# Splitting an image's projected rows during its own turned write pass

## The chip, the cores and the metric

The kernel runs on one core of a Trainium2 chip. The metric is the device time of one execution in microseconds (us); the three timed runs before the change give a median of 9846.35 us. One more execution was profiled: every start and duration quoted here comes from that one.

## What is computed

The input `x` is a batch of 8 images of 128x128 pixels with 128 channels. Layer 0 is a linear attention with a norm and a residual. Layer 1 is a block with a selective scan in four directions, cut here to what the change touches:

```python
xz = x @ Win                       # per pixel: 128 -> 512
xb, z = jnp.split(xz, 2, axis=-1)  # 256 channels each
xb = silu(conv3x3_depthwise(xb) + conv_b)
xf = xb.reshape(Bb, Cd, L)                               # natural order of pixels
xt = jnp.transpose(xb, (0, 1, 3, 2)).reshape(Bb, Cd, L)  # turned order
xs = jnp.stack([xf, xf[..., ::-1], xt, xt[..., ::-1]], axis=1)
x_dbl = jnp.einsum('bcl,cd->bdl', xs_flat, Wxproj)       # 256 channels -> 10 rows
dt, Bs, Cs = x_dbl[:, :8], x_dbl[:, 8:9], x_dbl[:, 9:]   # then the scan over L
```

L is 128*128 = 16384, Cd is 256. The scan needs, for each image, the silu output times B (in natural and in turned order), and the ten rows of `x_dbl` (in both orders).

## The kernel before, in words

The program has three stages on the same core, one after the other: `layer0`, `layer1_front` and `layer1_scan`. An all-engine barrier (line 713) stands between the second and the third. In the front and the scan stage `in_order` writes the order of every engine by hand: what the source calls first is first in that engine's queue, and nothing overtakes it. Nearly all DMAs are issued from SP (SyncE), in one queue.

`layer1_front` is the stage of the change. It goes over the 8 images in the order `SEQ` = 4, 6, 5, 7, 0, 1, 2, 3, and cuts each into 16 chunks of 8x128 = 1024 pixels, numbered g = 0 to 15 within the image (n over all images). `step(n)` interleaves neighbouring chunks: TensorE projects (`project`) and does two taps of the convolution (`taps_pe`), ScalarE does three taps (`taps_act`), GpSimd adds them (line 504), VectorE does the other taps (`taps_dve`, lines 510 and 512), and ScalarE applies silu into the resident tile `ures` (128 KB per partition: the whole image, both halves of the 256 channels). `rows` and `keep_rows` make the ten rows of a chunk and store them to `xds` in DRAM. `by_b` (line 549) multiplies `ures` by B and writes it in natural order. `load_sum`, `sum_d` and `store_sum` carry a sum over directions through DRAM (tile `gl`, tag `d`).

Between two images, at g = 0 of the next one, stands the turned write pass, `turn`: 32 pieces (2 channel halves of 16), each copied from `ures` with rows and columns exchanged into a tile `turned` of 128x1024 (line 622; 19 copies on VectorE, 13 on ScalarE), then written to DRAM by a DMA of 512 KB (line 623). The tiles come from two rings of buffers shared with other tiles of the stage: tag `tb` with four buffers and tag `tc` with two (every third piece). A ring hands out its buffers in the order of the calls: a new tile waits until everything that used the tile four (or two) places earlier is done, a DMA out of it included. The next image's silu overwrites `ures`, so the pass stands in every engine's path.

`split` handles half of an image's ten rows (five rows) at a time, from `load_rows`, which reads them back from `xds` as `xw`, 128x5x128, in runs of 512 B (640 of them). Five TensorE transposes (line 605, PSUM tag `pj`, one buffer, shared with `project`) and a ScalarE copy (line 607) make the turned version `xh`. `split3` (lines 43 and 45) then cuts each version into three bfloat16 parts on VectorE: cast, subtract, cast, subtract, cast. So one split has ten VectorE instructions of 128x640, and six DMAs of 160 KB to `xps` (line 613) in runs of 256 B. Before the change the two splits of an image are called at the end of the steps g = 1 and g = 2 of the next image, and the last image's two after the loop, ahead of the barrier.

Of the kernel before, what the change touches and what calls it, by code (L numbers as in the profile page):

```python
# [8 lines left out]
F32 = mybir.dt.float32  # L9
# [7 lines left out]
P = 128  # L17
B = 8
H = W = 128
L = H * W  # L20
NH, HD = 4, 32
NC2 = 2
# [7 lines left out]
CH = 1024  # L30
CW = CH // H
NCH = L // CH
# [4 lines left out]
NAT, TURN = 0, 1  # L37


def split3(nc, parts, x):  # L40

    for j in range(3):
        nc.vector.tensor_copy(parts[j], x)
        if j < 2:
            nc.vector.tensor_tensor(x, x, parts[j], ALU.subtract)
# [327 lines left out]
def layer1_front(ctx: ExitStack, tc, x1, win, conv_w, conv_b, wxp, d_par, ubs, xds, xps, gts, gs):  # L373
# [11 lines left out]
    nc = tc.nc  # L385
    const = ctx.enter_context(tc.tile_pool(name="l1c", bufs=1))
    big = ctx.enter_context(tc.tile_pool(name="l1b", bufs=1))
    wp = ctx.enter_context(tc.tile_pool(name="l1w", bufs=3))
# [34 lines left out]
    for j, d in enumerate(ON_PE):  # L423
        for c in range(NC2):
            dg = wp.tile([P, P], F32, name="dg1", tag="tb", bufs=4)
            nc.vector.tensor_scalar(dg, ident, cw[:, c, tap(*d) : tap(*d) + 1], None, ALU.mult)
            p = pm.tile([P, P], F32, name="pw", tag="m")
# [16 lines left out]
    uturn = ures.rearrange("p c (w h) -> p c h w", h=H)  # L444
# [3 lines left out]
    SEQ = (4, 6, 5, 7, 0, 1, 2, 3)  # L448

    def place_of(n):  # L450
        return SEQ[n // NCH % B], n % NCH
# [3 lines left out]
    def load(n):  # L455
        b, g = place_of(n)
        x = xins[n % 2]
        cols = CW + 1 if g < NCH - 1 else CW
        src = x1[b].rearrange("c (w h) -> c w h", h=H)[:, g * CW : g * CW + cols, :]
        nc.sync.dma_start(x[:, 0:cols, inner], src)  # L460
        if g == NCH - 1:
            nc.gpsimd.memset(x[:, CW, :], 0.0)

    def project(n, c):
        pxs[n, c] = px = pj.tile([P, CW, H], F32, name="pxb", tag="pj")
        for hf in range(2):
            nc.tensor.matmul(  # L467
                px[:, hf * 4 : hf * 4 + 4, :], wi[:, c, :], xins[n % 2][:, hf * 4 : hf * 4 + 4, inner],
                start=True, stop=True,
            )  # L470

    def place(n, c):

        g = n % NCH
        xb, old = xbs[n % 2], xbs[(n - 1) % 2]
        nc.scalar.copy(xb[:, c, 1 : CW + 1, inner], pxs.pop((n, c)))
        if g == 0:
            nc.gpsimd.memset(xb[:, c, 0, :], 0.0)
        else:
            nc.scalar.copy(old[:, c, CW + 1, inner], xb[:, c, 1, inner])  # L480
            nc.scalar.copy(xb[:, c, 0, inner], old[:, c, CW, inner])
        if g == NCH - 1:
            nc.gpsimd.memset(xb[:, c, CW + 1, :], 0.0)
# [4 lines left out]
    def taps_pe(n, c):  # L488
        accs[n, c] = acc = pa.tile([P, CW, H], F32, name="acc", tag="acc")
        for hf in range(2):  # L490
            s = slice(hf * 4, hf * 4 + 4)
            for j, (dw, dh) in enumerate(ON_PE):
                x = xins[n % 2][:, hf * 4 + dw : hf * 4 + dw + 4, 1 + dh : 1 + dh + H]
                nc.tensor.matmul(acc[:, s, :], wt[:, j, c, :], x, start=(j == 0), stop=(j == len(ON_PE) - 1))  # L494
# [13 lines left out]
    def taps_dve(n, c):  # L508
        acc = accs[n, c]
        nc.vector.tensor_tensor(acc, sums.pop((n, c)), acc, ALU.add)  # L510
        for d in ON_DVE:
            nc.vector.scalar_tensor_tensor(  # L512
                acc, at(n, c, *d), cw[:, c, tap(*d) : tap(*d) + 1], acc, ALU.mult, ALU.add
            )
# [15 lines left out]
    def keep_rows(n):  # L530
        b, g = place_of(n)
        t = xdt[n % 2]
        nc.scalar.copy(t[0:64, :], prs.pop(n))
        for hf in range(2):
            s = slice(g * CH + hf * 512, g * CH + hf * 512 + 512)
            nc.sync.dma_start(xds[b][:, s], t[32 * hf : 32 * hf + R + 2, :])

    def spread(n, hf):
        pbs[n, hf] = p = pm.tile([P, 1, 512], F32, name="pb", tag="m")
        nc.tensor.matmul(p[:, 0, :], bsel[:, hf, :], xdt[n % 2], start=True, stop=True)  # L540

    def by_b(n):

        b, g = place_of(n)
        dst = ubs[b, NAT].rearrange("c p l -> p c l")
        for hf in range(2):
            s = slice(g * CH + hf * 512, g * CH + hf * 512 + 512)
            u = ures[:, :, s]
            nc.vector.tensor_tensor(u, u, pbs.pop((n, hf)).to_broadcast([P, NC2, 512]), ALU.mult)
            nc.sync.dma_start(dst[:, :, s], u)  # L550

    def sums_at(n, c):
        b, g = place_of(n)
        i = NCH - 1 - g if b // 2 % 2 == 1 else g
        if b >= 4:
            return gts[b % 2, c, :, i].rearrange("p e q -> p (e q)")
        return gs[b % 2, c][:, i * CH : i * CH + CH]

    def load_sum(n, c):
        b, g = place_of(n)  # L560
        if b // 2 != 2:
            gls[n, c] = gl = wp.tile([P, CH], F32, name="gl", tag="d", bufs=2)
            if b // 2 == 0:
                nc.sync.dma_start(gl.rearrange("p (e q) -> p e q", e=NCH), gts[b % 2, c, :, :, g])
            else:
                nc.sync.dma_start(gl, sums_at(n, c))
# [21 lines left out]
    def store_sum(n, c):  # L588
        nc.sync.dma_start(sums_at(n, c), dus.pop((n, c)))

    half = (R + 2) // 2
    xws = {}

    def load_rows(b, i):
        r = slice(i * half, i * half + half)
        xws[b, i] = x = wp.tile([P, half, H], F32, name="xw", tag="tc", bufs=2)
        nc.sync.dma_start(x, xds[b].rearrange("r (w h) -> w r h", h=H)[:, r, :])

    def split(b, i):

        r = slice(i * half, i * half + half)
        x = xws.pop((b, i))
        pt = pj.tile([P, half, P], F32, name="ptx", tag="pj")
        for j in range(half):
            nc.tensor.transpose(pt[:, j, :], x[:, j, :], ident)
        y = wp.tile([P, half, W], F32, name="xh", tag="tc", bufs=2)
        nc.scalar.copy(y, pt)  # L607
        for order, v in ((TURN, y), (NAT, x)):
            q = wp.tile([P, 3, half, P], BF16, name="parts", tag="tb", bufs=4)
            split3(nc, [q[:, j] for j in range(3)], v)  # L610
            dst = xps[b, order].rearrange("j r (a e) -> a j r e", e=P)
            for j in range(3):
                nc.sync.dma_start(dst[:, j, r, :], q[:, j])

    def turn(dst):

        for c in range(NC2):
            for i in range(NCH):
                k = NCH * c + i
                t = wp.tile([P, CW, W], F32, name="turned", tag="tc" if k % 3 == 2 else "tb", bufs=2 if k % 3 == 2 else 4)  # L620
                copy = nc.scalar.copy if k % 5 in (1, 3) else nc.vector.tensor_copy
                copy(t, uturn[:, c, i * CW : i * CW + CW, :])
                nc.sync.dma_start(dst[c][:, i * CH : i * CH + CH], t.rearrange("p h w -> p (h w)"))

    def step(n):

        live, then, later, before = 0 <= n < N, 0 <= n + 1 < N, 0 <= n + 2 < N, 1 <= n <= N
        b, g = place_of(n)
        if live:
            taps_dve(n, 0)  # L630
        if before:
            keep_rows(n - 1)
        if then:
            project(n + 1, 1)
            place(n + 1, 1)
        if live:
            taps_pe(n, 1)
        if later:
            load(n + 2)
        if before:  # L640
            for c in range(NC2):
                store_sum(n - 1, c)
        if live:
            for c in range(NC2):
                load_sum(n, c)
        if before:
            for hf in range(2):
                spread(n - 1, hf)
        if before and g == 0:
            by_b(n - 1)  # L650
            turn(ubs[place_of(n - 1)[0], TURN])
        if then:
            taps_act(n + 1, 0)
        if live:
            silu(n, 0)
        if then:
            taps_pe(n + 1, 0)
        if later:
            project(n + 2, 0)
        if live:  # L660
            taps_dve(n, 1)
        if then:
            taps_act(n + 1, 1)
        if before and g != 0:
            by_b(n - 1)
        if live:
            silu(n, 1)
        if later:
            place(n + 2, 0)
        if live:  # L670
            rows(n)
            sum_d(n)
        if n >= NCH and g in (1, 2):
            split(place_of(n - NCH)[0], g - 1)
        if n >= NCH and g in (0, 1):
            load_rows(place_of(n - NCH)[0], g)

    with in_order(tc):
        for n in range(-2, N + 1):
            step(n)  # L680
        for i in range(2):
            if i == 1:
                load_rows(SEQ[-1], 1)
            split(SEQ[-1], i)


@with_exitstack
# [497 lines left out]
```

## Time and profile before

| what | us |
|---|---|
| three timed runs: lowest, median, highest | 9833.42, 9846.35, 9846.51 |
| the profiled execution, its own time | 9824.87 |
| its span (first to last instruction on the core) | 9823.0 |
| VectorE busy in the span | 8276.1 |
| ScalarE busy, GpSimd busy, TensorE busy | 7129.7, 7184.2, 6386.5 |
| front stage, first convolution step to the end of the last turned copy | 2391 to 4946 |
| first VectorE instruction behind the barrier | 4976.70 |

A row of the timeline reads: start, duration, engine, line, operation, output<-input, shapes, count, and in brackets how long the engine had been idle and what it waited for. Rows that follow one another on one line of code are merged. A row of the table by windows reads: the window, its length, busy time and number of instructions of each engine, the TensorE clock granted, the mean busy share of the 16 DMA engines (1.0 is full) and the bytes per second.

### The profile page before, as it was taken

How to read it: one execution, taken by the hardware profiler on the slowest of the kernel's cores; microseconds unless marked ns; L12 is line 12 of the kernel's file. 1: busy time of each engine (PE TensorE's matmuls, PEld its weight loads, DVE VectorE, ACT ScalarE, POOL GpSimd, SP SyncE). 2: the span in 40 equal slices, each digit the busy share in tenths (PEclk: the TensorE clock that was granted, in tenths of full speed). 3: DMA queues.
4: the chain of work that ended last, by engine and by line, in shares of the span. 5: the costliest groups of instructions: out<-in, count | busy, mean ns of one | idle time of the engine just before them, and what ended most of it. 6: DMA issues, size and time to landing. Idle time of an engine off the chain costs nothing. (4 is left out here: it accounts for less than half of the span.)

```text
span 9823.0 us, 89967 instructions
## 1 busy us (share of the span) xinstructions
PE 6386.5 (65%) x24352; PEld 3135.3 (32%) x24352; DVE 8276.1 (84%) x8676; ACT 7129.7 (73%) x8226; POOL 7184.2 (73%) x4352
## 2 busy tenths in 40 slices
PE   8999999988787678667823544636345363553636
PEld 5555555553232223222300311404123040220403
DVE  6557775566898889888979999999999999999996
ACT  5556565556887788777778788887877878787784
POOL 3444554455484578667759899898998989889897
PEclk9999999999898889888955765757557585665857
DMA  2332233323666678877664957759587684866858
GB/s 91 129 131 97 86 118 131 129 101 132 219 221 214 219 265 228 243 248 263 232 197 152 253 177 202 234 164 263 154 223 207 176 257 152 246 185 191 239 153 215
DMA packets 1034807, 1851.21 MB, mean 188 GB/s; under 512 B 274852, under 2 KB 500772, under 8 KB 1026112
## 3 DMA queue, kind: packets, MB, share of 16 engines
q1 hardware_dynamic: 999488, 1711.23, 53.4%
q0 software_dynamic: 34816, 134.23, 7.1%
q8 instruction: 199, 3.26, 0.1%
q14 instruction: 304, 2.49, 0.1%
HBM read 1153.03 MB, written 692.12 MB: 188 GB/s over the span
## 5 line engine op out<-in xcount | busy, mean ns | idle before, releaser
L882 POOL TENSOR_TENSOR ubt<-ubt,sp 128x1024 f32<-128x1024 f32 x1024 | 2451.4, 2441 | 186.3 <-ACT sp L875 159.5
L871 PE MATMUL px<-rows,dtw 128*128 128x512 bf16 x2048 | 948.3, 564 | 2251.9 <-DVE y L941 1011.9
L504 POOL TENSOR_TENSOR tap<-tap 128x1024 f32<-128x1024 f32 x512 | 1206.2, 2366 | 720.7 <-ACT tap L502 614.7
L512 DVE SCALAR_TENSOR_TENSOR acc<-xb,cw,acc 128x1024 f32<-128x1024 f32 x1024 | 1320.7, 1290 | 51.1
L494 PE MATMUL acc<-xi,wt 128*128 128x512 f32 x2048 | 984.3, 625 | 570.8 <-ACT ures L519 570.5
L875 ACT ACTIVATE sp<-px 128x1024 f32<-128x1024 f32 x1024 | 1035.0, 1023 | 405.8 <-PE px L871 263.8
L948 POOL TENSOR_TENSOR y<-y,ubt 128x512 f32<-128x512 f32 x768 | 1160.6, 1548 | 146.4 <-DVE ubt L922 142.8
L871 PEld LDWEIGHTS <-dtw 128*128 128x128 bf16 x2048 | 167.5, 110 | 3071.4 <-issue 963.9
L889 DVE TENSOR_TENSOR_SCAN ubt<-px,state,ubt 128x1024 f32<-128x1024 f32 x480 | 1106.0, 2335 | 4.9 <-issue 3.6
L891 DVE TENSOR_TENSOR_SCAN ubt<-px,state,ubt 128x1024 f32<-128x1024 f32 x480 | 1104.6, 2335 | 6.0 <-issue 3.6
L879 ACT ACTIVATE px<-sp,sa 128x1024 f32<-128x1024 f32 x1024 | 1103.3, 1109 | 6.1
L502 ACT ACTIVATE tap<-xb,cw 128x1024 f32<-128x1024 f32 x768 | 833.2, 1139 | 155.4 <-DVE acc L510 92.4
L875 ACT ACT_TABLE_LOAD x512 | 656.9, 1283 | 223.7 <-PE px L871 205.8
L274 POOL TENSOR_TENSOR q<-q,qs 128x512 f32<-128x512 f32 x256 | 270.9, 1058 | 674.0 <-DVE qs L273 672.8
L494 PEld LDWEIGHTS acc<-xi,wt 128*128 128x128 f32 x2048 | 395.8, 199 | 1139.0 <-ACT ures L519 676.0
L879 ACT ACT_TABLE_LOAD x512 | 656.9, 1283 | 9.0
L1013 PEld LDWEIGHTS px<-wg,z 128*128 128x128 f32 x4096 | 586.3, 228 | 163.9 <-issue 157.9
L905 PE MATMUL pc<-rows,csel 128*128 128x512 bf16 x1024 | 515.9, 584 | 128.0 <-DVE rstd L1001 125.2
L1013 PE MATMUL px<-wg,z 128*128 128x128 f32 x4096 | 585.3, 312 | 0.0
L467 PE MATMUL pxb<-xi,wi 128*128 128x512 f32 x1024 | 497.4, 608 | 29.1 <-ACT xh L607 24.7
L941 DVE TENSOR_TENSOR y<-y,px 128x1024 f32<-128x1024 f32 x384 | 468.6, 1220 | 14.2
L922 DVE TENSOR_TENSOR ubt<-ubt,pc 128x1024 f32<-128x1024 f32 x384 | 466.2, 1214 | 0.0
(158 smaller groups left out, 15026.4 us busy)
## 6 DMA issues: line engine op xcount, KB each, us to landing
ubt<-ubs SPq DMA_DIRECT2D x512, 1024.0 KB
zs<-z SPq DMA_DIRECT2D x512, 256.0 KB
ubs<-ures SPq DMA_DIRECT2D x256, 512.0 KB
ubs<-turned SPq DMA_DIRECT2D x256, 512.0 KB
y<-gs POOLq DMA_DIRECT2D x128, 1024.0 KB, 11.9
z<-zs SPq DMA_DIRECT2D x256, 512.0 KB
rows<-xps SPq DMA_DIRECT2D x1536, 60.0 KB
xi<-x SPq DMA_DIRECT2D x120, 576.0 KB
```

What stands on the lines that cost most here:

```text
L494: nc.tensor.matmul(acc[:, s, :], wt[:, j, c, :], x, start=(j == 0), stop=(j == len(ON_PE) - 1))
L502: nc.scalar.activation(t, at(n, c, *d), AF.Copy, scale=cw[:, c, tap(*d) : tap(*d) + 1])
L504: nc.gpsimd.tensor_tensor(sums[n, c], sums[n, c], t, ALU.add)
L512: nc.vector.scalar_tensor_tensor(acc, at(n, c, *d), cw[:, c, tap(*d) : tap(*d) + 1], acc, ALU.mult, ALU.add)
L871: nc.tensor.matmul(p[:, hf * 512 : hf * 512 + 512], sl.dw[:, c * P : c * P + P], src, start=True, stop=True)
L875: nc.scalar.activation(t, da[n, c], AF.Softplus)
L879: nc.scalar.activation(da[n, c], sp[n, c], AF.Exp, scale=sa[:, sl.s, c : c + 1])
L882: nc.gpsimd.tensor_tensor(ubt[n][:, c, :], ubt[n][:, c, :], sp.pop((n, c)), ALU.mult)
L889: nc.vector.tensor_tensor_scan(e[:, ::-1], x[:, ::-1], e[:, ::-1], start, ALU.mult, ALU.add)
L891: nc.vector.tensor_tensor_scan(e, x, e, start, ALU.mult, ALU.add)
L948: nc.gpsimd.tensor_tensor(v[:, c], v[:, c], h[:, c], ALU.add)
L1013: nc.tensor.matmul(po[:, w, :], z[:, c, w * H : w * H + H], wg[:, c, :], start=(c == 0), stop=(c == NC2 - 1))
```

## The change

`turn` becomes `leave(b)`. It first calls `load_rows` for both halves of the image that it is about to write, then makes the same 32 pieces, and calls `split(b, 0)` behind piece 9 and `split(b, 1)` behind piece 19. The calls of `load_rows` and `split` at the end of the steps, and the code behind the loop, go. Two buffers move with it: `xw` uses the ring `d` (two buffers, that of `gl`) and `xh` the ring `tb`; `parts` stays in `tb`. Because `xw` now holds the ring `d` during the pass, `load_sum` of the step g = 0 is called after the pass and no longer ahead of it. The number of instructions, their shapes and the bytes moved are the same.

```diff
     def load_rows(b, i):
         r = slice(i * half, i * half + half)
-        xws[b, i] = x = wp.tile([P, half, H], F32, name="xw", tag="tc", bufs=2)
+        xws[b, i] = x = wp.tile([P, half, H], F32, name="xw", tag="d", bufs=2)
         nc.sync.dma_start(x, xds[b].rearrange("r (w h) -> w r h", h=H)[:, r, :])
...
-        y = wp.tile([P, half, W], F32, name="xh", tag="tc", bufs=2)
+        y = wp.tile([P, half, W], F32, name="xh", tag="tb", bufs=4)
...
-    def turn(dst):
-
-        for c in range(NC2):
-            for i in range(NCH):
-                k = NCH * c + i
-                t = wp.tile([P, CW, W], F32, name="turned", tag="tc" if k % 3 == 2 else "tb", bufs=2 if k % 3 == 2 else 4)
-                copy = nc.scalar.copy if k % 5 in (1, 3) else nc.vector.tensor_copy
-                copy(t, uturn[:, c, i * CW : i * CW + CW, :])
-                nc.sync.dma_start(dst[c][:, i * CH : i * CH + CH], t.rearrange("p h w -> p (h w)"))
+    def leave(b):
+
+        for i in range(2):
+            load_rows(b, i)
+        for k in range(NC2 * NCH):
+            c, i = divmod(k, NCH)
+            t = wp.tile([P, CW, W], F32, name="turned", tag="tc" if k % 3 == 2 else "tb", bufs=2 if k % 3 == 2 else 4)
+            copy = nc.scalar.copy if k % 5 in (1, 3) else nc.vector.tensor_copy
+            copy(t, uturn[:, c, i * CW : i * CW + CW, :])
+            nc.sync.dma_start(ubs[b, TURN][c][:, i * CH : i * CH + CH], t.rearrange("p h w -> p (h w)"))
+            if k % 10 == 9 and k < 20:
+                split(b, k // 10)
...
-        if live:
+        if live and g != 0:
             for c in range(NC2):
                 load_sum(n, c)
...
         if before and g == 0:
             by_b(n - 1)
-            turn(ubs[place_of(n - 1)[0], TURN])
+            leave(place_of(n - 1)[0])
+        if live and g == 0:
+            for c in range(NC2):
+                load_sum(n, c)
...
-        if n >= NCH and g in (1, 2):
-            split(place_of(n - NCH)[0], g - 1)
-        if n >= NCH and g in (0, 1):
-            load_rows(place_of(n - NCH)[0], g)
 
     with in_order(tc):
         for n in range(-2, N + 1):
             step(n)
-        for i in range(2):
-            if i == 1:
-                load_rows(SEQ[-1], 1)
-            split(SEQ[-1], i)
```

## The prediction, made before the changed kernel was seen

> **What bounds the kernel now.** I read the page first, then the timeline of VectorE around the end of an image, then the table by windows, then the tail of the stage.
>
> ```profile
> span 9823.0 us, 89967 instructions
> ...
> PE 6386.5 (65%) x24352; PEld 3135.3 (32%) x24352; DVE 8276.1 (84%) x8676; ACT 7129.7 (73%) x8226; POOL 7184.2 (73%) x4352
> ```
>
> VectorE (DVE) has most work, but a share over the span says nothing of one stage, so I look at the front alone. First VectorE in the first image, where no split is called, then at the same place of the second image, where one is:
>
> ```profile
> 2404.57 1.23 DVE L510 TENSOR_TENSOR acc<-tap,acc 128x1024 f32<-128x1024 f32 x1 [0.33 <-PE acc L494]
> ...
> 2413.44 1.23 DVE L510 TENSOR_TENSOR acc<-tap,acc 128x1024 f32<-128x1024 f32 x1 [2.28 <-PE acc L494]
> ...
> 2419.95 2.35 DVE L549 TENSOR_TENSOR ures<-ures,pb 128x1024 f32<-128x1024 f32 x2
> 2422.21 1.22 DVE L510 TENSOR_TENSOR acc<-tap,acc 128x1024 f32<-128x1024 f32 x1
> ```
> ```profile
> 2717.53 2.35 DVE L549 TENSOR_TENSOR ures<-ures,pb 128x1024 f32<-128x1024 f32 x2
> 2723.24 1.08 DVE L43 CAST parts<-xh 128x640 bf16<-128x640 f32 x1 [3.37 <-issue]
> 2724.35 2.86 DVE L45 TENSOR_TENSOR xh<-xh,parts 128x640 f32<-128x640 f32 x1
> 2727.24 0.49 DVE L43 CAST parts<-xh 128x640 bf16<-128x640 f32 x1
> 2727.77 0.82 DVE L45 TENSOR_TENSOR xh<-xh,parts 128x640 f32<-128x640 f32 x1
> ...
> 2732.27 1.22 DVE L510 TENSOR_TENSOR acc<-tap,acc 128x1024 f32<-128x1024 f32 x1
> ```
>
> Without a split VectorE goes from by_b (L549) straight into the next step's taps (L510): VectorE is the bound of a chunk step. With one, 12.4 us lie between (2719.9 to 2732.3): 3.4 idle and the ten instructions, some stretched. The time from one step's first L510 to the next one's gives the price of it. Image 0: 17.6 for g = 1 (with the 2.28 wait on TensorE above), then 15.3 in every step. The seven later images: g = 1 takes 30.1, 27.5, 30.1, 31.2, 31.2, 30.1, 30.1; g = 2 takes 29.0, 25.7, 29.3, 29.5, 29.7, 29.1, 29.1; g = 3 15.2; g = 4 15.6 to 16.7.
>
> The turned pass is bound otherwise:
>
> ```profile
> core 0: us, PE busy (x) PEld busy (x) DVE busy (x) ACT busy (x) POOL busy (x), PEclk, DMA share, GB/s
> 2645.00:2692.00 47.00, 0.00 (x0) 0.00 (x0) 21.86 (x22) 25.05 (x14) 0.00 (x0) 0.51 1.01 397
> 2970.00:3010.00 40.00, 0.00 (x0) 0.00 (x0) 20.48 (x21) 23.99 (x13) 0.00 (x0) 0.50 1.03 419
> ```
> ```profile
>   DMA ubs<-turned: 287.0, 197
> ```
>
> DMA share is 1: the pass is the DMA's. VectorE works half of it, GpSimd and TensorE not at all; the second fence (what ended the idle time ahead of the turned copies) says that 197 copies waited 287 us for a buffer's write to land. The tail of the stage, last turned copy to first instruction behind the barrier, holds the last image's splits alone:
>
> ```profile
> 4943.68 1.91 ACT L622 COPY turned<-ures 128x1024 f32<-128x1024 f32 x1 [2.01 <-DMA ubs<-turned]
> 4947.26 1.22 SPq L597 DMA_DIRECT2D xw<-xds  x1
> 4953.19 0.93 PEld L605 LDWEIGHTS ptx<-ident,xw 128*128 128x128 f32 x5 [49.10 <-DMA xw<-xds]
> ...
> 4976.70 0.07 DVE L741 MEMSET half<- 128x8 f32 x1 [2.41 <-SPq L713]
> ```
>
> **What the Trainium skill says.** "SBUF — State Buffer", section "Who interferes with whom": a VectorE instruction with two SBUF inputs contends with a GpSimd instruction that reads SBUF. The trace agrees: the same subtraction takes 2.86 us while GpSimd adds the sums, 0.82 when it does not. In the pass GpSimd is idle, so I take the short times there. "DMA: Bandwidth & Descriptors", section "Where 436 GB/s comes from", puts the ceiling of the 16 DMA engines at 435 GB/s; the pass shows 419. The same page, "Specifications", wants 512 B or more in a run for full rate; the parts are written in runs of 256 B. The trace agrees, and prices it: in the window 4966 to 4977, with six such DMAs and little else, the DMA share is 0.35 of 11.0 us, so 3.85 us, 0.64 each, or 256 GB/s.
>
> **The change, part by part.**
>
> 1. The splits leave the chunk steps. What g = 1, 2 and 4 took above 17.6, 15.3 and 15.3 is 26.5, 21.6, 27.0, 29.1, 29.4, 26.7 and 26.7: **187 us** gone. What is late next is VectorE itself, in back-to-back taps, as in image 0; the restart after the pass (TensorE after silu) stays. Least gain: the VectorE instructions alone, 14 splits of 8.5 (line totals 52.8+32.7+26.4+23.6 over 16), 119.
>
> 2. The tail. The last copy ends at 4945.6, the scan starts at 4976.7: 31.1. Left in it is the landing of the last pieces and the barrier. The load queued right behind the last piece reached TensorE at 4953.2, and takes some 1.5 itself, so the last piece landed near 4951.5; with 0.8 for the barrier 6.8 stay: **24 us** gone (22 to 26).
>
> 3. load_sum moves behind the pass. Before, it waits in SP's queue until the step before's store has landed (5.5 us from issue to issue at the first boundary), and all turned writes queue behind it. From by_b's end to the last copy's end the eight passes take 46.7, 41.0, 46.8, 46.8, 46.2, 43.7, 46.3 and 38.7; the second and the last have no load_sum. At 41.0 all seven in the loop save **30 us**. Not all of it is safe: load_rows now needs the same two buffers, and at the four boundaries that leave an image with such a sum waits for the same stores. There the DMA has the step's input, two stores and by_b's writes queued, some 6.7 us, so I put the wait at nothing; uncovered, it is up to 3.6 each, 14. Its own late arrival costs nothing by my count: issued at the end of the pass, behind some 5 us of writes, it lands 8 to 10 us after the last copy, and GpSimd wants it at 14.5 (2706.4 against 2691.9). With that cover gone it would cost 3 to 5 at six boundaries, 24 at most.
>
> 4. The pass takes the splits in. The two loads are 320 KB each; the window 4963.5 to 4966, which holds one, has share 0.46 of 2.5, so 1.12: 2.2 for two, on the DMA, ahead of the first piece. SP issues them in 0.5 to 1.2 each while by_b's writes still run. The transposes stand on an idle TensorE early in the pass; behind them on it is nothing until the next silu. A split's six writes are 3.85 of DMA: the floor. Above it, the DMA runs dry. I walk the ring from the landing of piece 4 as time 0, a piece each 1.25: xh takes piece 4's buffer and is copied by ScalarE (0.67) at 0.8; the first parts tile takes piece 6's, free at 2.5; five VectorE instructions (three of 0.49, two of 0.83, with gaps 3.2) end at 5.7, the other five, in piece 7's buffer, at 8.9; only then can VectorE copy piece 10 (1.03), for the copies are in order, and SP issues in order, so piece 11, ready on ScalarE, waits too. From copy to first byte is some 1.5, so piece 10 is on the DMA from 11.5 to 12.8, where before it was done at 7.0. Pieces up to 9 keep the DMA busy until 5.8; the six writes follow with gaps, as VectorE makes one each 1.3, and end near 11. A split so costs **5.8 us**; the same walk at piece 19 gives the same. Both ends: 3.85 (all else hidden), and 10.4 if the DMA is dry for the whole split (0.67, ten instructions 6.24 and gaps, 3.0 from a first issue to its landing, 4908.1 to 4911.1). I take 5.8, since backlog covers the beginning. Eight times (2.2 + 11.6) is **110 us** added.
>
> Sum: -187 - 24 - 30 + 110 = -131. Against the profiled execution's own time (span 9823.0, 1.9 around it, 9824.9) that is 9694; the median of the timed runs lies 21.5 higher, so I take 131 off the median: **9716**.
>
> **Rivals.** (a) The write pass empties at each split (10.4 each): 74 more, 9790. For it: three of the four tb buffers are taken at once, and 197 copies already wait for a landing. Against: the ring holds some 4 us of writes when it starts. (b) The end on the other side: besides running dry, the refill waits for the parts' own landings, since the ring gives their two buffers to pieces 13 and 15. From issue to landing under load is some 5.3, so a split costs 15.7, and the sum is -241 + 8 x (2.2 + 31.4) = +28: 9874. It decides from 14 a split on. Against it: the six writes are only 3.85 of DMA, and land before piece 12 is copied in my walk. (c) The steps g = 1 and 2 stay long, because what slows them is partly the restart after the pass and not the split: half of the 187 stays, 9808. Against it: image 0, with the same 2.28 wait, needs no more than 17.6. (d) The splits' writes hide fully, floor 3.85: 31 less, 9685, or less still.
>
> **Chances.** Forecast 0.74 (9680 to 9770), (a) 0.12, (b) 0.05, (c) 0.05, (d) beyond 9680 0.04. The low end is the floor of the splits; the high end takes splits at 8 (+35) and the uncovered waits for stores (+14). A measurement of this kernel can tell about 0.2%, 20 us, from no change. Slower by that: (b), 0.04; within it 0.03; faster 0.93.
>
> **What would show it.** Steps g = 1 and 2 at 17.6 and 15.3 in all images; the passes near 55 us from by_b's end to the last copy, with DMA share near 0.9 and gaps at two places, where L43 and L45 take 0.49 and 0.83; the barrier some 7 us after the last copy. It is wrong if the passes take over 66, if the steps behind them stay above 20, or if GpSimd waits for gl in g = 0.

## The result, and the profile after

The changed kernel takes 9714.4 us in the median (9691.45 to 9720.68, 4 runs), beside 9839.9 us for the kernel before: a ratio of 0.9869 with a 95% interval of 0.9849 to 0.9888. The forecast was 9716 (9680 to 9770). The profiled execution has a span of 9689.7 us, 133.3 less than before.

```profile
span 9689.7 us, 89952 instructions
...
PE 6369.1 (66%) x24352; PEld 3134.8 (32%) x24352; DVE 8237.5 (85%) x8676; ACT 7126.3 (74%) x8226; POOL 7180.5 (74%) x4352
```

The engines have the same instructions. VectorE is busy 38.6 us less; 35.4 of that is in lines 43 and 45, the split's instructions, which are no longer stretched beside GpSimd. The rest of the 133 us was idle time. VectorE's timeline at the place that was shown of the second image before:

```profile
2717.88 1.23 DVE L510 TENSOR_TENSOR acc<-tap,acc 128x1024 f32<-128x1024 f32 x1 [2.28 <-PE acc L494]
...
2724.38 2.35 DVE L549 TENSOR_TENSOR ures<-ures,pb 128x1024 f32<-128x1024 f32 x2
2726.64 1.22 DVE L510 TENSOR_TENSOR acc<-tap,acc 128x1024 f32<-128x1024 f32 x1
```

By_b runs straight into the next taps, with the 2.28 wait of image 0. The same split now stands in the pass (line 623 is the turned copy, 622 before):

```profile
2657.29 1.03 DVE L623 COPY turned<-ures 128x1024 f32<-128x1024 f32 x1 [1.38 <-DMA ubs<-turned]
2660.93 0.49 DVE L43 CAST parts<-xh 128x640 bf16<-128x640 f32 x1 [2.61 <-DMA ubs<-turned]
2661.46 0.83 DVE L45 TENSOR_TENSOR xh<-xh,parts 128x640 f32<-128x640 f32 x1
...
2666.95 0.49 DVE L43 CAST parts<-xw 128x640 bf16<-128x640 f32 x1
2667.36 3.83 DVE L623 COPY turned<-ures 128x1024 f32<-128x1024 f32 x4
```

The first cast waits for a turned piece to land (the ring), then ten instructions run at 0.49 and 0.83, and the next piece is copied 6.4 us after the split began. What the DMA does meanwhile is in the table by windows, one microsecond at a time (the last two columns are DMA share and GB/s):

```profile
2662.00:2663.00 1.00, 0.00 (x0) 0.00 (x0) 0.93 (x3) 0.00 (x0) 0.00 (x0) 0.50 1.05 430
2663.00:2664.00 1.00, 0.00 (x0) 0.00 (x0) 0.96 (x2) 0.00 (x0) 0.00 (x0) 0.50 0.98 370
2664.00:2665.00 1.00, 0.00 (x0) 0.00 (x0) 0.90 (x3) 0.00 (x0) 0.00 (x0) 0.50 1.18 274
2665.00:2666.00 1.00, 0.00 (x0) 0.00 (x0) 0.97 (x2) 0.00 (x0) 0.00 (x0) 0.50 0.95 221
2666.00:2667.00 1.00, 0.00 (x0) 0.00 (x0) 0.93 (x3) 0.53 (x1) 0.00 (x0) 0.50 0.57 148
2667.00:2668.00 1.00, 0.00 (x0) 0.00 (x0) 1.00 (x2) 1.00 (x1) 0.00 (x0) 0.50 0.63 163
2668.00:2669.00 1.00, 0.00 (x0) 0.00 (x0) 1.00 (x2) 0.42 (x1) 0.00 (x0) 0.50 0.49 131
2669.00:2670.00 1.00, 0.00 (x0) 0.00 (x0) 1.00 (x2) 0.00 (x0) 0.00 (x0) 0.50 0.92 348
2670.00:2671.00 1.00, 0.00 (x0) 0.00 (x0) 1.00 (x2) 0.00 (x0) 0.00 (x0) 0.50 0.98 401
```

Turned pieces fill the DMA until 2663.8, the six small writes follow, with a share of one half to two thirds for three microseconds, and turned pieces run again from 2669.1. That is 5.3 us for the split; the same reading at the second split gives 5.4. The share can exceed 1.0 in this view (1.18 in one row), so 1.0 is not its upper end. Whole passes, by the same table:

```profile
2643.00:2698.00 55.00, 2.63 (x10) 1.86 (x10) 33.60 (x42) 26.36 (x16) 0.00 (x0) 0.53 0.97 359
2950.00:3004.00 54.00, 2.63 (x10) 1.86 (x10) 32.89 (x41) 26.07 (x16) 0.00 (x0) 0.50 0.98 362
```

The tail, from the last turned copy to the first instruction behind the barrier (line 739 is the 741 of before), is 6.65 us long:

```profile
4834.86 1.92 ACT L623 COPY turned<-ures 128x1024 f32<-128x1024 f32 x1 [1.92 <-DMA ubs<-turned]
4843.43 0.07 DVE L739 MEMSET half<- 128x8 f32 x1 [8.84 <-SPq L711]
```

Where the time went, from the two timelines:

| part | before | after | difference | forecast |
|---|---|---|---|---|
| eight passes, by_b's end to last copy's end | 356.1 | 434.4 | +78.3 | +80 |
| g = 1 to 4 of the seven later images | 630.7 | 444.3 | -186.4 | -187 |
| restart: last copy to the first taps of g = 1, and the taps of g = 0 ahead of the pass | 139.3 | 140.9 | +1.6 | 0 |
| tail | 31.1 | 6.65 | -24.4 | -24 |
| last chunk and all other steps | 1428.5 | 1427.8 | -0.7 | 0 |
| ahead of the front | 2391.1 | 2389.5 | -1.6 | 0 |
| behind the barrier | 4846.3 | 4846.2 | -0.1 | 0 |

### The profile page after: what moved, and what is told of

It is laid out like the page before. It is cut to its first block, busy times and chain, and to the rows that moved or that the text cites. A ratio compares the mean times of both kernels' runs of the same rounds, so it can differ in the third digit from the quotient of the medians.

```text
span 9689.7 us, 89952 instructions
## 1 busy us (share of the span) xinstructions
PE 6369.1 (66%) x24352; PEld 3134.8 (32%) x24352; DVE 8237.5 (85%) x8676; ACT 7126.3 (74%) x8226; POOL 7180.5 (74%) x4352
## 3 DMA queue, kind: packets, MB, share of 16 engines
q1 hardware_dynamic: 999488, 1711.23, 54.2%
## 5 line engine op out<-in xcount | busy, mean ns | idle before, releaser
L494 PE MATMUL acc<-xi,wt 128*128 128x512 f32 x2048 | 952.7, 608 | 383.5 <-ACT ures L519 383.1
L290 ACT ACTIVATE sq<-o 128x512 f32<-128x512 f32 x256 | 161.2, 630 | 421.6 <-DVE o L288 420.4
```

## The experiments

The front's beginning lies between 2389 and 2403 us in the executions below, though the code ahead of it is the same. So traces are compared by the length of the front (first taps to first instruction behind the barrier): 2585.6 before, 2454.0 in the changed kernel.

**load_sum moved, and nothing else.** The kernel before with

```diff
-        if live:
+        if live and g != 0:
             for c in range(NC2):
                 load_sum(n, c)
...
             turn(ubs[place_of(n - 1)[0], TURN])
+        if live and g == 0:
+            for c in range(NC2):
+                load_sum(n, c)
```

> The kernel before, with load_sum of g = 0 called behind the turned pass and nothing else changed. My theory (the wait of load_sum for the last step's store holds up SP, and with it the turned writes): all seven passes inside the loop take 41.0 us from by_b's end to the last copy's end, where they took 41.0 to 46.8; steps and tail stay; 30 us less than before, 0.3%. Rival (the DMA has other work during that wait, or the late load comes back as GpSimd's wait for gl): 0 to 8 us less.

Measured: 9806.0 us, ratio 0.9967 (0.9957 to 0.9978). The seven passes in the loop take 40.9 to 41.5 (29 us less together; the last is 1 longer), the front is 2551.3, 34 less. SP's queue shows the pass begin straight behind by_b's writes, and the load behind it:

```profile
2653.93 1.06 SPq L589 DMA_DIRECT2D gts<-du  x2
2655.61 2.05 SPq L550 DMA_DIRECT2D ubs<-ures  x2
2657.87 41.04 SPq L623 DMA_DIRECT2D ubs<-turned  x32
2698.96 2.48 SPq L566 DMA_DIRECT2D gl<-gts  x2
```

So about a quarter of the change's gain comes from a line that looks like a mere consequence of sharing a buffer ring.

**No split at all.** The changed kernel without the calls of `load_rows` and `split`, and with one DMA of zeros to `xps` in the step g = 8. It leaves the bfloat16 parts out: the scan reads zeros in their place.

```diff
-        for i in range(2):
-            load_rows(b, i)
...
-            if k % 10 == 9 and k < 20:
-                split(b, k // 10)
...
+            if g == 8:
+                fill(b)
```

> The changed kernel without load_rows and split: the bfloat16 parts are left out, and zeros are written in their place by one DMA of 2 MB in the step g = 8 of each image, where the DMA is busy about two thirds. Theory: the passes fall to 41.0 us (39 for the last), 13.4 less each, 107 us less than the changed kernel, about 240 less than before; steps 17.6 and 15.3. Rival (part of the pass's length is not the splits but the wait for buffers or stores at its start): passes stay above 44, less than 85 us gained over the changed kernel.

Measured: 9612.7 us, ratio 0.9772 (0.9757 to 0.9787). Passes 40.8 to 41.5, the last 38.6: 108 us less than in the changed kernel, and the front is 2353.7, 100 less (the steps with the zeros take some 8 us more in all). So everything above 41 in the changed kernel's passes, 13.5 us an image, is the splits, their loads and what these loads wait for. Of such waits for stores nothing shows: the changed kernel's passes that leave images 6, 7 and 2, where a store may still read the buffers that load_rows needs, take 54.2 to 54.7, the other four in the loop 54.5 to 54.9.

**Splits cut in two.** The changed kernel with the turned parts of a half made behind pieces 7 and 19 and the natural parts behind 13 and 25:

```diff
...
-            if k % 10 == 9 and k < 20:
-                split(b, k // 10)
+            if k in (7, 13, 19, 25):
+                split(b, k // 14, TURN if k % 12 == 7 else NAT)
```

> The changed kernel, with each split cut in two: the turned parts behind pieces 7 and 19, the natural parts behind 13 and 25. Theory (a split costs its writes, 3.85 us of DMA, and on top some 1.5 to 2 in which the DMA runs dry, since VectorE copies no piece for 6.2 us): 3.1 us of VectorE at a time hide under the writes queued, the passes go from 54.4 to about 51 us, 25 us less than the changed kernel, 156 to 160 less than before. Rival (the cost is the 256-byte writes themselves, dry or not): passes stay at 54, time as the changed kernel. Second rival (each cut ties up the buffer ring anew): passes get longer, 56 to 60.

Measured: 9691.7 us, ratio 0.9852 (0.9839 to 0.9865). Passes 52.9 to 53.3, the last 51.3: 11 us less together, not 25; the front is 2438.8, 15 less. There was dry time, and most of it has gone, but it was smaller than the theory had it. A pass of this kernel, and one of the kernel without splits:

```profile
2651.00:2705.00 54.00, 2.63 (x10) 1.86 (x10) 35.12 (x44) 26.74 (x16) 0.00 (x0) 0.53 1.01 371
2654.00:2695.00 41.00, 0.00 (x0) 0.00 (x0) 21.37 (x21) 24.86 (x14) 0.00 (x0) 0.53 1.03 416
```

The DMA share of the pass is 1.01 here and 1.03 where there is no split; over the seven passes in the loop it is 1.00 and 1.03. So the DMA is nearly as full as without splits, and about 52 us (an estimate: 53.15 times 1.002 over 1.029) and not 51 is what the pass would take with the DMA equally full.

**The changed kernel once more, and three other places.** With it ran: the second split behind the last piece, and the first behind piece 21; the half splits behind 7, 12, 20 and 25, each ahead of a piece that ScalarE copies; and the same with the turned rows split in PSUM.

> The changed kernel once more, on the chip of the three kernels below: some 125 to 133 us less than before (ratio 0.987), passes 54.2 to 54.9 us.

Measured: 9710.5 us, ratio 0.9871 (0.9854 to 0.9887), passes 54.3 to 55.1, front 2455.0.

```diff
-            if k % 10 == 9 and k < 20:
-                split(b, k // 10)
+            if k in (21, 31):
+                split(b, k // 31)
```

> The changed kernel with the splits behind pieces 21 and 31 (the last one) in place of 9 and 19. Theory: the second split's writes no longer stand ahead of a turned piece, so the passes lose its 5.3 us (to about 49); its VectorE instructions fall into the 6 us in which VectorE waits for TensorE behind the pass, but silu of the second half comes later by some 2.4 us, and gl lands 3.85 us later: 2 to 3 us an image are gained, 16 to 24 in all, less some 5 at the barrier. Rival (VectorE's taps, next in its queue, are late by the whole split, and all that follows): nothing gained or up to 10 us lost.

Measured: 9737.5 us, ratio 0.9897 (0.9882 to 0.9911): 27 us more than the changed kernel on the same chip, where a gain was expected and the rival had at most 10 us lost. The passes do fall, to 48.7 to 49.5, but the restart takes 60 us more in seven images, g = 1 some 1.4 each, and the tail 4. VectorE behind the last piece:

```profile
2708.04 0.49 DVE L43 CAST parts<-xh 128x640 bf16<-128x640 f32 x1 [4.16 <-DMA ubs<-turned]
...
2711.35 0.49 DVE L43 CAST parts<-xw 128x640 bf16<-128x640 f32 x1
2711.94 2.94 DVE L45 TENSOR_TENSOR xw<-xw,parts 128x640 f32<-128x640 f32 x1
2714.92 2.52 DVE L43 CAST parts<-xw 128x640 bf16<-128x640 f32 x1
...
2718.74 1.22 DVE L510 TENSOR_TENSOR acc<-tap,acc 128x1024 f32<-128x1024 f32 x1
```

GpSimd's adds of the next chunk start at 2711.86 and stretch two of the instructions to 2.9 and 2.5 us, and the taps queued behind begin 10.7 us after the split's first cast. The idle time behind the pass that was to hide the split lies behind those taps, not ahead of them.

```diff
-            if k in (7, 13, 19, 25):
-                split(b, k // 14, TURN if k % 12 == 7 else NAT)
+            if k in (7, 12, 20, 25):
+                split(b, k // 14, TURN if k in (7, 20) else NAT)
```

> The kernel with four half splits, now behind pieces 7, 12, 20 and 25, so that the piece behind each is one that ScalarE copies while VectorE makes the parts. Theory (what is left above the writes' own DMA time is the wait for VectorE's next copy): passes fall from 53.1 to about 51.5, 10 us less in all than with 7, 13, 19, 25. Rival (it is the gaps between the three writes themselves, one each 1.3 us): within 3 us of it.

Measured: 9688.4 us, ratio 0.9849 (0.9834 to 0.9863). Passes 53.1 to 54.5, front 2442.0: no shorter than with 7, 13, 19 and 25. The theory falls; the front is 3 us from that kernel's, about as the rival had it, but that does not show the rival's cause.

```diff
-            v = wp.tile([P, half, W], F32, name="xh", tag="tb", bufs=4)
-            nc.scalar.copy(v, pt)
+            v = pt
```

> The same, with the turned rows split where they lie in PSUM: no xh copy and one buffer of the ring fewer taken, but casts of 0.82 us in place of 0.49 as in the kernel with parts from PSUM. Theory (VectorE's time is what makes the writes late): a turned half takes 4.1 us of VectorE for 3.1, passes 0 to 2 us longer than with the copy. Rival (the ring is what binds): passes 1 to 3 us shorter.

Measured: 9694.9 us, ratio 0.9853 (0.9838 to 0.9867). Passes 52.9 to 53.1, front 2435.7. Shorter than the kernel before it by 0.6 us a pass in the trace, and not to be told from it in time. Neither theory is borne out.

**The writes themselves.** Two edits of the last kernel: the third part's write issued first; and the second split's parts kept in the ring `tc` and written behind the last piece, with turned pieces from 20 on in the ring `tb` alone.

```diff
-            for j in range(3):
+            for j in (2, 0, 1):
                 nc.sync.dma_start(dst[:, j, r, :], q[:, j])
```

> The kernel of quarters from PSUM, with the third part's write issued ahead of the first two, so that the three go out together once VectorE is done. If gaps between the writes are what is left above their DMA time, passes fall by some 1.5 us (51.5), 12 us less in all; if the DMA is full already, they stay at 53 or grow by up to 1.5.

Measured: 9698.4 us, ratio 0.9862 (0.9849 to 0.9876), passes 54.3 to 55.6, 1.7 longer. Sending the three writes together does not shorten the pass. It also makes the first two later, so it does not show by itself that gaps between the writes cost nothing.

```diff
...
+            tag, bufs = ("tc", 2) if i else ("tb", 4)
+            q = wp.tile([P, 3, half, P], BF16, name="parts", tag=tag, bufs=bufs)
...
             for j in range(3):
-                nc.sync.dma_start(dst[:, j, r, :], q[:, j])
+                held.append((dst[:, j, r, :], q[:, j]))
+            if i == 0:
+                send()
...
-            t = wp.tile([P, CW, W], F32, name="turned", tag="tc" if k % 3 == 2 else "tb", bufs=2 if k % 3 == 2 else 4)
+            t = wp.tile([P, CW, W], F32, name="turned", tag="tc" if k % 3 == 2 and k < 20 else "tb", bufs=2 if k % 3 == 2 and k < 20 else 4)
...
                 split(b, k // 14, TURN if k in (7, 20) else NAT)
+        send()
```

> The kernel of quarters with the turned rows in PSUM; the second split's two parts tiles now lie in the ring tc, which no turned piece uses from piece 20 on, and their six writes are issued behind the last piece, so that they run beside the next chunks. Theory (the pass is the DMA's, so only what is taken out of its queue shortens it): the passes lose 3.85 us each, 53.0 to about 49.2, unless the four buffers that are left from piece 20 on are too few for the 5.3 us from issue to landing; gl lands 3.85 later, which is still covered but for 1 us; 20 to 28 us less than with quarters from PSUM, 165 to 175 less than before. Rival (what leaves the pass comes back behind it, as in the kernel with the second split last): within 8 us of the kernel with quarters from PSUM. Second rival (four buffers starve the DMA): passes stay at 52 to 55.

Measured: 9685.1 us, ratio 0.9847 (0.9834 to 0.9861), passes 50.9 to 51.9, front 2429.2, the shortest of those that make the parts. Of the 3.85 us that the six writes take, 1.5 a pass came off. The packet records show where the rest went: in a pass 3840 packets of 256 B fewer take 3.85 us less, as the theory had it, but 240 more packets of 4 KB (4100 for 3860) take 2.2 more. With four buffers in place of six at the end, some two more pieces must have landed before the last copy can start. In the first pass the DMA share also falls to 0.69 and 0.55 in two single microseconds near the end. The four kernels with cut splits and the writes in their natural order, 9685 to 9695, have overlapping intervals, with one another and with the changed kernel. Their medians lie below both of the changed kernel's and their fronts are 12 to 26 us shorter, but time alone settles neither their order nor how much they gain.

**What stretched the splits before.** The kernel before, with the turned rows split where they lie in PSUM:

```diff
-        y = wp.tile([P, half, W], F32, name="xh", tag="tc", bufs=2)
-        nc.scalar.copy(y, pt)
-        for order, v in ((TURN, y), (NAT, x)):
+        for order, v in ((TURN, pt), (NAT, x)):
```

> The kernel before, with the turned rows left where TensorE writes them: split3 works on ptx in PSUM, the copy xh is gone, so the subtraction has one SBUF input only. If the stretched instructions (2.86 us beside GpSimd, 0.82 alone) come from the port that VectorE shares with GpSimd for a second SBUF input, the subtractions of the turned half fall from a mean of 1.65 to about 0.85 us, and steps g = 1 and 2 lose some 2 to 4 us each: 30 to 50 us less than before in all. If the stretch has another cause (waiting for the first cast's result, for instance), the first subtraction stays above 2 us and the time stays within 15 us.

Measured: 9789.4 us, ratio 0.9950 (0.9937 to 0.9964), front 2536.2, 49 less than before. The instructions of line 45, counts, and shortest, median and longest duration in ns:

```profile
L45 DVE TENSOR_TENSOR ptx<-ptx,parts x32: 832/833/833, 2726.9 to 4925.2; 128x640 f32<-128x640 f32 x32
```

Before, the same row of the subtraction on `xh` ran from 824 to 3365, with a mean of 1651. The 12 of them that ran beside GpSimd's adds had a mean of 3.03 us, the other 20 of 0.83. With one input in PSUM all 32 take 0.83, and 24 of these ran beside GpSimd's adds. So waiting for the first cast's result is excluded. That the second SBUF input is what stretched them agrees with the Trainium skill ("SBUF — State Buffer", section "Who interferes with whom"), but the edit also moves the subtraction's result into PSUM, and no run separates the two.

Of the 49 us only 11.5 are busy time of lines 43 and 45: the subtractions lose 26.2, while the casts from PSUM take 6.9 more and casts of `xw`, which now fall beside the adds, 7.8 more. Most of the rest is idle time of VectorE ahead of the splits, 73 us before and 40 here: the copy `xh` on ScalarE is gone, and the first cast no longer waits for it (3.37 us idle before it at the place shown of the second image, 1.66 here).

## Why the prediction was right

Each term came out near its forecast, as the table shows. That the median lies within 2 us of the forecast is luck in part: the four times spread over 29 us, and beside the median of before in the same comparison the gain is 125.5 us, where 131 was forecast.

1. The splits out of the chunk steps, 187: measured 186.4. The control inside the kernel before, image 0 without a split, gave 17.6 and 15.3 for g = 1 and 2, and all seven images now have exactly these. Counting VectorE's instructions alone, the lower end, would have given 119: the price is read from the period of the steps, not from the busy time of what goes.

2. The tail, 24: measured 24.4.

3. load_sum behind the pass, 30: measured alone, 28 in the eight passes and 34 in the front. The working's own numbers, 3 to 5 us at six boundaries, make at most 30 and not 24 for a late arrival that is not covered. It was covered: in the changed kernel GpSimd waited 9.0 us for gl in all, before 3.5, and none of these waits lies at the add of g = 0 behind a pass. The restart is 1.6 longer than before, but with load_sum moved alone it is 136.9, shorter than the 139.3 of before, so the late load does not explain it; what does is not shown.

4. The splits in the pass, 110: the passes end near 54.5, as the forecast had it, and without splits at 41. Of the 13.5 us an image, two splits are 10.7 (walked: 11.6) and the rest, 2.8, are the loads and what else the pass gained (forecast: 2.2). The walk was right in its order: first cast behind a landing, next piece behind the ten instructions. From the first cast the last turned bytes before the writes end 3.3 us later and the next copy starts 6.4 us later (first split), in the walk as in the trace. It was 0.5 too long a split because it had 2.6 from the start of that copy to its first bytes (1.03 and 1.5), where the packet records show 1.9 at all 16 splits.

What was wrong: the table by windows was to show a share near 0.9 in the passes; it shows 0.97. I had the dry time as 1.9 a split. The trace shows 5.3 us for writes that the DMA records price at 3.95 (7680 packets of 256 B in the pass, 16.5 ns each on average, over 16 engines), so 1.4. And in the kernel with cut splits, where the DMA is nearly as full as without splits, a pass takes 12.0 us more than without splits (53.15 and 41.11, means of the seven in the loop), where the forecast has 2.2 for the loads and 7.7 for the writes. The packet records of the two traces show what the other 2 us are. The writes take 7.8 and the loads 2.2, as forecast. The 4 KB packets, most of them of turned pieces, take 163.6 ns each in place of 160.0, which is 0.8 us a pass. About 1 us is the share, 1.00 in place of 1.03. The forecast took the turned pieces' own rate as unchanged.

Rival (a), a dry DMA for the whole split, and (b), a refill held up by the parts' own landings, are not what happened, though a trace of (b) is there: eight copies waited for a parts write to land, 39.8 us in all.

```profile
  DMA ubs<-turned: 221.8, 116
  DMA xps<-parts: 39.8, 8
```

These rows are from the list of what ended the idle time ahead of the turned copies. There is one such wait in each pass, of the copy of piece 11 on ScalarE. That copy ended 0.04 to 0.43 us after VectorE's copy of piece 10 (2668.42 and 2668.38 in the first pass), and piece 10 stands ahead of it in SP's queue, so no piece was held up by it that the trace shows. Rival (c), a slow restart in g = 1 and 2, is excluded by the steps. Rival (d), splits at the floor of their writes, 3.85, does not hold either: they cost 5.3, and cutting them in two brings them nearer to it.

## What to carry to other kernels

A stage that the DMA bounds can take in work for the other engines, but not free of charge: price what the moved step puts into the DMA queue (here 13.5 us an image for 26.6 us taken out of a stage that VectorE bounds), and look for a place where the step already does not occur, which gives its price in the old place. Moving the same split a little further, to the end of the same pass, lost 27 us, because its instructions then stood ahead of the taps and beside GpSimd again. When an edit moves a second thing for the sake of a buffer, test it alone: load_sum's move gave a quarter of the gain.

## What the runs showed of the hardware

A cast to bfloat16 of 128x640 takes VectorE 0.49 us from SBUF and 0.82 us from PSUM. Beside GpSimd's adds a cast from SBUF to SBUF was held up as well (2.52 us; the Trainium skill, in the same section of "SBUF — State Buffer", names casts among the instructions that can take the port pair shared with GpSimd), and a subtraction with one of its inputs and its result in PSUM was not (0.83). The small writes cost nearly the same in a full queue as alone: a packet of 256 B took 15.8 ns on average before the change, between 4966 and 4977 with little else on the DMA, and 16.4 among the turned pieces. The larger packets beside them grew more in sum: those of 4 KB took 160.0 ns in the passes without splits and 163.6 in those with cut splits.
